# Layer 0 of a four-layer graph network: the set-up and the block chains of the scatter places in small steps, matmuls and adds one turn behind their inputs

## The chip, the cores and the metric

The kernel runs on one core of a Trainium2 chip. The metric is the device time in microseconds of one execution; three runs of the kernel before give 11480.86 us as the median (11465.4 to 11503.06).

## The reference

Four graph layers over 6250 nodes with 128 features and 200000 edges. Each layer normalizes the nodes, gathers rows by one end of an edge, and sums what it made of them at the other end. Layer 0, which the change touches:

```python
h = jnp.maximum(_layernorm(x, axis=-1), 0.0)
agg = jax.ops.segment_sum(h[src], dst, num_segments=6250)     # edge_index = stack([src, dst])
x = x + jax.nn.relu((h + agg) @ W1 + b1) @ W2 + b2
```

Edges come sorted by `dst`. Layer 1 sums by `src` instead, so its messages must be put in the order of `src`.

## The kernel before

**The windows of layer 0** (`windows0`, L795 to L832). The edges are cut into NG = 391 groups of FT = 4 tiles of 128. As `dst` is sorted, a group touches a window of at most FW = 64 nodes. For each group g, POOL gathers four tiles of rows of `h_tab` by `src` with indirect DMAs (`gather`, L298) into one of the buffers of `m` (pool `eg`, 6); DVE makes the one-hot rows of the edges' places in the window (`hot`, L822); PE adds up the group with four f32 matmuls, eight passes in the profile (`ps`, L825, 3 PSUM buffers); and DVE adds `ps` into `acc` at the window's start (L827), which it has in a register that is loaded for eight groups at a time (`starts`, L608).

**The places for layer 1** (`ranks`, L613 to L793) are computed in the same stretch. It is a Python generator: after each group, `windows0` calls it for a number of turns (L828): one for g below 20, then two and three by turns. It finds for each edge its place in a stable order by `src // 32` (NB = 196 bins), as follows. (1) Constants and shifted ids. (2) Fourteen turns that count all bins: each makes two wide one-hot tiles `hot_h` (L663, 128 x 1792) and has 14 matmuls on them (L666). (3) Steps on small tiles: the counts are folded, go through memory (`c_tab`, L690 and L691), are scanned (L694), and give each group's first bin (L707 to L728), with matmuls between. (4) 820 turns over the 782 pairs of tiles. `sums(q)` makes the pair's one-hot rows `hot_b` (L744, two DVE instructions) and adds them into the block's `sizes` with a matmul (L746). A block is RB = 32 pairs. After its last pair, `before_tiles` (L749 to L772) runs the block's chain in one turn: DVE copies the sizes (L752, L753), PE makes the counts before each tile and the running total (L755 to L762), DVE splits them into three bf16 pieces (L764 to L771). `places(q)` comes 38 turns after `sums(q)`: PE makes the pair's places in PSUM (`pq`, L778 and L779, 2 buffers), and DVE picks and sums each row's own with `hot_b` (L782, two instructions with a read of the sum after each).

**What sets the order.** Each engine works through its own queue in order. The framework orders instructions when the program is built, near the order of the source, and inserts the waits. In the built program DVE has L827 of a group behind the L782 of the group's first turn and ahead of the L744 of its second; PE has a pair's L746 two turns behind its L744, just ahead of a later pair's L778.

Of the kernel before, what the change touches and what calls it, by code (L numbers as in the profile page):

```python
# [9 lines left out]
F32 = mybir.dt.float32  # L10
I32 = mybir.dt.int32
BF16 = mybir.dt.bfloat16
# [8 lines left out]
D = 128  # L21
# [34 lines left out]
def bcast(col, n):  # L56

    p, g = col.shape
    return col.unsqueeze(2).to_broadcast([p, g, n])
# [9 lines left out]
def gnn_kernel(ctx: ExitStack, tc: tile.TileContext, t, out):  # L69
# [543 lines left out]
    def ranks(st, src):  # L613
# [6 lines left out]
        bp = st.enter_context(tc.tile_pool(name="rb", bufs=RB + RLAG + 2))  # L620
        wp = st.enter_context(tc.tile_pool(name="rw", bufs=3))
        qp = st.enter_context(tc.tile_pool(name="rq", bufs=1, space=PSUM))
        rp = st.enter_context(tc.tile_pool(name="rr", bufs=2, space=PSUM))
# [3 lines left out]
        sh = kp.tile([P, n], I32, name="sh")  # L627
# [30 lines left out]
        yield  # L658
        count = qp.tile([P, HK, 16], F32, name="count")
        for b in range(0, n8, HN):  # L660
            hot = hp.tile([P, 2, HN, 16], BF16, name="hot_h")
            for k in range(2):
                nc.vector.tensor_tensor(hot[:, k], lanes[:, :16].unsqueeze(1).to_broadcast([P, HN, 16]),  # L663
                                        bcast(parts[:, k, b:b + HN], 16), op=ALU.is_equal)
            for i in range(0, HN, HK):
                nc.tensor.matmul(count, hot[:, 0, i:i + HK, :].rearrange("p k l -> p (k l)"),  # L666
                                 hot[:, 1, i:i + HK, :].rearrange("p k l -> p (k l)"),
                                 start=(b + i == 0), stop=(b + i == n8 - HK))
            yield
# [8 lines left out]
        nc.vector.tensor_scalar(mask, lanes[:, :HK], own_f[:, 0:1], None, op0=ALU.is_equal)  # L678
        diag = kp.tile([P, HK, 16], F32, name="diag")
# [3 lines left out]
        fold = kp.tile([P, 16], F32, name="fold")  # L683
        nc.vector.tensor_scalar(fold, lanes[:, :16], own_f[:, 1:2], None, op0=ALU.is_equal)
        pr = qp.tile([16, 16], F32, name="count")
        nc.tensor.matmul(pr, fold, by_hi, start=True, stop=True)
        sizes = kp.tile([16, 16], F32, name="sizes")
        nc.vector.tensor_copy(sizes, pr)
        cr = kp.tile([1, 3, NB], F32, name="cr")
        nc.sync.dma_start(c_tab[0].rearrange("(h l) -> h l", l=16), sizes)  # L690
        nc.sync.dma_start(cr[:, 0, :], c_tab[0:1, 0:NB])  # L691
        yield
        nc.vector.memset(cr[:, 2, :], 0.0)
# [4 lines left out]
        nc.tensor.matmul(pr, ones[0:1, :], cr[:, 1, :], start=True, stop=True)  # L698
        ends = kp.tile([P, NB], F32, name="ends")
        nc.vector.tensor_copy(ends, pr)  # L700
        bin_ = kp.tile([P, 2, 4], F32, name="bin_")
        for k in range(2):
            for c in range(4):
                le = wp.tile([P, NB], F32, name="junk")
                at = wp.tile([P, 1], F32, name="at")
                nc.vector.tensor_scalar(at, pid, float(FE), float(c * P * FE + k * (FE - 1)), op0=ALU.mult,
                                        op1=ALU.add)  # L707
                nc.vector.tensor_scalar(le, ends, at, None, op0=ALU.is_le)
                nc.vector.tensor_reduce(bin_[:, k, c:c + 1], le, axis=AX.X, op=ALU.add)
        yield  # L710
        by_group = kp.tile([1, 2, 4 * P], F32, name="by_group")
        for k in range(2):
            pr = qp.tile([1, 4 * P], F32, name="count")
            for c in range(4):
                nc.tensor.matmul(pr[:, c * P:(c + 1) * P], bin_[:, k, c:c + 1], ident, start=True, stop=True)
            nc.vector.tensor_copy(by_group[:, k, :], pr)
# [9 lines left out]
        nc.tensor.matmul(pr, ones[0:1, :], by_group[:, 0, :NG], start=True, stop=True)  # L726
        nc.vector.tensor_copy(base_b, pr)
        yield  # L728
        pos_f = kp.tile([P, n], F32, name="pos_f")
        sofar = cr[:, 2, :]  # L730
        hots, pieces = {}, {}
# [4 lines left out]

        def sums(q):

            b, i = divmod(q, RB)
            if i == 0:  # L740
                hots["ps"] = qp.tile([RB, 2, NB], F32, name="sizes")
            hot = hots[q] = bp.tile([P, 2, NB], BF16, name="hot_b")
            for k in range(2):
                nc.vector.tensor_scalar(hot[:, k, :], lanes_b, bins[:, 2 * q + k:2 * q + k + 1], None,  # L744
                                        op0=ALU.is_equal)
            nc.tensor.matmul(hots["ps"], at_pair[:, RB - i:2 * RB - i], hot, start=(i == 0),  # L746
                             stop=(i == RB - 1 or q == n // 2 - 1))

        def before_tiles(b, sofar):  # L749

            c = hp.tile([RB, 2, NB], F32, name="c")
            nc.vector.tensor_copy(c[:, 0, :], hots["ps"][:, 0, :])  # L752
            nc.vector.tensor_tensor(c[:, 1, :], c[:, 0, :], hots["ps"][:, 1, :], op=ALU.add)  # L753
            pb = qp.tile([3 * RB, 2, NB], F32, name="before")
            nc.tensor.matmul(pb, earlier[:, 0].rearrange("p k q -> p (k q)"), twice(c[:, 1, :]), start=True,  # L755
                             stop=False)
            nc.tensor.matmul(pb, ones[0:1, :3 * RB], twice(sofar), start=False, stop=False)
            nc.tensor.matmul(pb[:, 1, :], earlier[:, 1].rearrange("p k q -> p (k q)"), c[:, 0, :],
                             start=False, stop=True)
            pt = qp.tile([1, NB], F32, name="count")  # L760
            nc.tensor.matmul(pt, ones[:RB, 0:1], c[:, 1, :], start=True, stop=False)
            nc.tensor.matmul(pt, ones[0:1, 0:1], sofar, start=False, stop=True)  # L762
            sofar = hp.tile([1, NB], F32, name="sofar")
            nc.vector.tensor_copy(sofar, pt)  # L764
            r = hp.tile([3 * RB, 2, NB], F32, name="r")
            v = pieces[b] = hp.tile([3 * RB, 2, NB], BF16, name="pieces")
            nc.vector.tensor_copy(v, pb)
            nc.vector.scalar_tensor_tensor(r, v, part[:, 0:1], pb, op0=ALU.mult, op1=ALU.add)
            nc.vector.tensor_copy(v, r)
            nc.vector.scalar_tensor_tensor(r, v, part[:, 1:2], r, op0=ALU.mult, op1=ALU.add)  # L770
            nc.vector.tensor_copy(v, r)  # L771
            return sofar  # L772

        def places(q):
            b, i = divmod(q, RB)
            hot = hots.pop(q)
            pq = rp.tile([P, 2, NB], F32, name="pq")
            nc.tensor.matmul(pq, pick[:, i:i + 1].to_broadcast([3 * RB, P]), pieces[b], start=True, stop=False)  # L778
            nc.tensor.matmul(pq, below, hot, start=False, stop=True)  # L779
            for k in range(2):  # L780
                junk = wp.tile([P, NB], F32, name="junk")
                nc.vector.tensor_tensor_reduce(junk, pq[:, k, :], hot[:, k, :], 1.0, 0.0, ALU.mult, ALU.add,  # L782
                                               pos_f[:, 2 * q + k:2 * q + k + 1])

        for q in range(n // 2 + RB + RLAG):
            if q < n // 2:
                sums(q)
            if q % RB == RB - 1 and q < n // 2 or q == n // 2 - 1:
                sofar = before_tiles(q // RB, sofar)
            if 0 <= q - RB - RLAG:  # L790
                places(q - RB - RLAG)
            yield
        nc.vector.tensor_copy(pos, pos_f)  # L793

    def windows0():  # L795

        with ExitStack() as st:
# [3 lines left out]
            with ExitStack() as st:  # L801
                lp = st.enter_context(tc.tile_pool(name="ld", bufs=1))
                gp = st.enter_context(tc.tile_pool(name="eg", bufs=6))
                wp = st.enter_context(tc.tile_pool(name="ew", bufs=4))
                pp = st.enter_context(tc.tile_pool(name="ep", bufs=3, space=PSUM))
# [3 lines left out]
                di = lp.tile([P, NG * FT], I32, name="di")  # L809
                nc.sync.dma_start(di, t["dst_f"])  # L810
                loc = lp.tile([P, NG, FT], F32, name="loc")
                nc.vector.tensor_copy(loc, di.rearrange("p (g j) -> p g j", j=FT))
                nc.vector.tensor_tensor(loc, loc, bcast(base, FT), op=ALU.subtract)
# [3 lines left out]
                for g in range(NG):  # L817
                    m = gp.tile([P, FT, D], F32, name="m")
                    for j in range(FT):
                        gather(m[:, j, :], h_tab, src[:, g * FT + j:g * FT + j + 1])  # L820
                    hot = wp.tile([P, FT, FW], F32, name="hot")
                    nc.vector.tensor_tensor(hot, lane, bcast(loc[:, g, :], FW), op=ALU.is_equal)  # L822
                    ps = pp.tile([P, FW], F32, name="ps")
                    for j in range(FT):
                        nc.tensor.matmul(ps, m[:, j, :], hot[:, j, :], start=(j == 0), stop=(j == FT - 1))  # L825
                    a = acc[:, bass.ds(starts(g, DVE), FW)]
                    nc.vector.tensor_tensor(a, a, ps, op=ALU.add)  # L827
                    for _ in range(1 if g < 20 else 3 if g % 2 else 2):  # L828
                        next(rank, None)
                for _ in rank:  # L830
                    pass
# [745 lines left out]
```

## Time and profile before

| | us |
|---|---|
| runs: median (lowest to highest) | 11480.9 (11465.4 to 11503.1) |
| the profiled execution | 11639.2, span 11637.5 |
| layer 0's windows: first gather to last add L827 | 78.1 to 2457.5 |
| last L782 of the places | 2235.3 |
| TensorE clock granted over the span | 0.54 |

Busy time, engine by engine (share of the span, instructions), and the span in 40 slices of 291 us, each digit a busy share in tenths:

```profile
PE 8422.1 (72%) x32097; PEld 6515.2 (56%) x32097; DVE 5839.1 (50%) x23079; ACT 1506.2 (13%) x3279; POOL 6132.0 (53%) x6269
...
PE   3788888659998889989983666666663466566666
...
DVE  4455555323343434344434666666665355555555
...
PEclk9555555555555555555555555555555555655555
```

Layer 0's windows are the first eight slices or so: PE is at seven to eight tenths, no engine at nine, and after the first slice the granted clock is half. A row of the profile has the line, the engine, what it writes and reads, the count, and then the busy time, the mean in ns, the idle time just ahead of it on its engine, and what ended most of that. "Issue" is idle time with no wait that the profile shows; "remote" is a wait whose end the profile can't put down to an instruction of this core. Queue entries (POOLq, SPq) are not counted as busy.

### The profile page before, as it was taken

Reading aid. Unit: us, or ns where it says so; the run is one execution under the profiler, and the core shown is the slowest. Engines: PE = TensorE matmul, PEld = TensorE weight load, DVE = VectorE, ACT = ScalarE, POOL = GpSimd, SP = SyncE. Lnnn points to the kernel's source line nnn. Section 1 sums busy time; section 2 is a strip of 40 time slices with the busy share of each in tenths; the row PEclk is TensorE's granted clock in tenths of the full one; section 3 lists DMA queues with packets and bytes.
Section 4 is the critical chain, followed back from the end, with each engine's and each line's share of the span. In section 5 each row is a group of like instructions: output and inputs, shape, how many; then the busy total and the mean of one; then the engine's idle time right before and its main releaser. Section 6 shows DMA issues by size and latency. Waiting matters only on the chain.

```text
span 11637.5 us, 118951 instructions
## 1 busy us (share of the span) xinstructions
PE 8422.1 (72%) x32097; PEld 6515.2 (56%) x32097; DVE 5839.1 (50%) x23079; ACT 1506.2 (13%) x3279; POOL 6132.0 (53%) x6269
## 2 busy tenths in 40 slices
PE   3788888659998889989983666666663466566666
PEld 2444444446666556669953666666663465555555
DVE  4455555323343434344434666666665355555555
ACT  0000000014343334331110000000001010011101
POOL 5666666625665666640006555555551556555662
PEclk9555555555555555555555555555555555655555
DMA  2111111113333333335512222222221233333332
GB/s 65 44 44 44 44 43 44 44 55 93 93 93 92 95 92 95 93 104 158 158 64 60 65 66 64 65 66 63 66 63 62 80 88 88 86 86 88 88 87 81
DMA packets 457356, 893.32 MB, mean 77 GB/s; under 512 B 149642, under 2 KB 231743, under 8 KB 455763
## 3 DMA queue, kind: packets, MB, share of 16 engines
q1 hardware_dynamic: 245552, 456.89, 14.0%
q0 software_dynamic: 200192, 412.80, 12.6%
q10 hardware_dynamic: 10918, 15.65, 0.4%
q8 instruction: 281, 4.60, 0.2%
q14 instruction: 413, 3.38, 0.1%
HBM read 753.95 MB, written 130.80 MB: 76 GB/s over the span
## 4 chain that ended last, share of the span: by engine, by line
PE 30%; issue 8%; DVE 8%; another core or an unknown queue 8%; POOL 4%; ACT 1%; DMA 1%; DVEq 0%; ACTq 0%; POOLq 0%; SPq 0%
PE ps L959 6%; PE pz L1354 4%; PE pz L1073 4%; POOL m L298 4%; PE ps L1401 4%; PE ps L1153 3%; PE pw L905 1%; PE pf L896 1%; PE py L899 1%; DVE z L1358 1%; DVE z L1078 1%; PE ps L1154 1%; PE ps L1402 1%; DVE hot L1396 1%
## 5 line engine op out<-in xcount | busy, mean ns | idle before, releaser
L298 POOL DMA_INDIRECT m<-l_tab,src x1564 | 1522.2, 973 | 1242.7 <-issue 563.1
L302 POOL DMA_INDIRECT m_tab<-m,pos x1564 | 1569.4, 1003 | 1152.5 <-issue 576.2
L298 POOL DMA_INDIRECT m<-g_tab,dst x1564 | 1499.6, 959 | 1068.0 <-PE ps L1401 426.4
L298 POOL DMA_INDIRECT m<-h_tab,src x1564 | 1538.5, 984 | 849.5 <-issue 412.2
L1401 PE MATMUL ps<-hot,m 128*128 128x64 f32 x3128 | 736.7, 399 | 676.5 <-DVE hot L1396 351.8
L1153 PE MATMUL ps<-hot,m 128*128 128x64 f32 x3128 | 787.9, 420 | 486.6 <-issue 265.6
L1401 PEld LDWEIGHTS ps<-hot,m 128*128 128x128 f32 x3128 | 685.8, 310 | 720.3 <-DVE hot L1396 368.6
L1153 PEld LDWEIGHTS ps<-hot,m 128*128 128x128 f32 x3128 | 724.2, 327 | 550.0 <-issue 295.3
L1073 PE MATMUL pz<-win,hotT 65*128 65x128 f32 x3128 | 825.2, 441 | 277.9 <-DVE hotT L1070 136.8
L1354 PE MATMUL pz<-win,hotT 128*128 128x128 f32 x3128 | 786.7, 415 | 275.1 <-issue 183.9
L825 PEld LDWEIGHTS ps<-hot,m 128*128 128x128 f32 x3128 | 736.1, 326 | 391.9 <-issue 177.6
L899 PEld LDWEIGHTS py<-win,hotT 64*128 64x128 f32 x3128 | 676.2, 316 | 478.6 <-issue 426.3
L825 PE MATMUL ps<-hot,m 128*128 128x64 f32 x3128 | 732.5, 410 | 264.9 <-DVE hot L822 116.5
L909 DVE TENSOR_TENSOR m<-pw,L_gnn_b_f_b 128x512 f32<-128x512 f32 x391 | 269.7, 690 | 1259.6 <-PE pw L905 382.7
L905 PEld LDWEIGHTS pw<-L_gnn_W_f,sp_r 128*128 128x128 f32 x3128 | 683.9, 321 | 380.7 <-issue 334.3
L905 PE MATMUL pw<-L_gnn_W_f,sp_r 128*128 128x128 f32 x3128 | 800.6, 435 | 121.7 <-DVE sp_r L931 86.1
L1073 PEld LDWEIGHTS pz<-win,hotT 65*128 65x128 f32 x3128 | 713.4, 330 | 308.2 <-issue 153.9
L899 PE MATMUL py<-win,hotT 64*128 64x128 f32 x3128 | 785.4, 428 | 118.8 <-issue 106.3
L1354 PEld LDWEIGHTS pz<-win,hotT 128*128 128x128 f32 x3128 | 673.8, 308 | 298.4 <-issue 276.2
L896 PE MATMUL pf<-row_a,L_gnn_W_f 20*128 20x512 f32 x782 | 770.3, 1090 | 37.2 <-ACT sp_r L918 15.0
L959 PE MATMUL ps<-hot,m 128*128 128x64 f32 x3128 | 671.0, 420 | 18.7 <-DMA m<-m_tab 18.4
L959 PEld LDWEIGHTS ps<-hot,m 128*128 128x128 f32 x3128 | 671.4, 333 | 21.0 <-ACT ids L962 18.7
(315 smaller groups left out, 11881.8 us busy)
## 6 DMA issues: line engine op xcount, KB each, us to landing
m<-m_tab SPq DMA_DIRECT2D x391, 262.0 KB
row<-in_dst_row SPq DMA_DIRECT2D x390, 256.0 KB
row<-e_tab SPq DMA_DIRECT2D x390, 256.0 KB
row_w<-in_w_row SPq DMA_DIRECT2D x195, 256.0 KB
m<-h_tab,src POOLq DMA_INDIRECT x1564
m_tab<-m,pos POOLq DMA_INDIRECT x1564
m<-l_tab,src POOLq DMA_INDIRECT x1564
m<-g_tab,dst POOLq DMA_INDIRECT x1564
```

What stands on the lines that cost most here:

```text
L298: nc.gpsimd.indirect_dma_start(out=dst, out_offset=None, in_=table[:], in_offset=bass.IndirectOffsetOnAxis(ap=idx, axis=0))
L302: nc.gpsimd.indirect_dma_start(out=table[:], out_offset=bass.IndirectOffsetOnAxis(ap=idx, axis=0), in_=src, in_offset=None, **kw)
L825: nc.tensor.matmul(ps, m[:, j, :], hot[:, j, :], start=(j == 0), stop=(j == FT - 1))
L896: nc.tensor.matmul(pf, w_f1, row["a"][:, es], start=True, stop=True)
L899: nc.tensor.matmul(py[:, j, :], hot[:, j * P:(j + 1) * P], w, start=True, stop=True)
L905: nc.tensor.matmul(pw[:, j, :], sp[:, j * P:(j + 1) * P], w_f2, start=True, stop=True)
L909: nc.vector.tensor_tensor(v, pw, b_f2b.unsqueeze(1).to_broadcast([P, FT, D]), op=ALU.add)
L959: nc.tensor.matmul(ps, m[:, j, :D], hot[:, j, :], start=(j == 0), stop=(j == FT - 1))
L1073: nc.tensor.matmul(pz[:, j, :], hot[:, j * P:(j + 1) * P], w, start=True, stop=True)
L1153: nc.tensor.matmul(ps[:, 0, :], m[:, j, :], hot[:, j, :], start=(j == 0), stop=(j == FT - 1))
L1354: nc.tensor.matmul(pz[:, j, :], hot[:, j * P:(j + 1) * P], w, start=True, stop=True)
L1401: nc.tensor.matmul(ps[:, 0, :], m[:, j, :], hot[:, j, :], start=(j == 0), stop=(j == FT - 1))
```

## The change

Nothing is computed in another way; steps move between turns, and buffers change.

- `windows0`: in iteration g, POOL's gathers and `hot` of group g, then the turns, then the matmuls of group g - 1, then the add of group g - 2; two iterations more. `eg` 7 buffers instead of 6, `ps` 2 instead of 3. One turn up to g = 35 instead of 19. The `dst` ids land in `loc` itself, and the cast ahead of the subtraction (L812) is gone.
- Set-up: constants (`fold`, the eight `at` columns, the zeroed row of `cr`) move ahead of the counting; the counting's matmuls are a turn behind their `hot_h`; the small steps stand in 12 turns instead of 3, with three turns between the two table DMAs and the scan.
- Pairs: DVE makes `hot_b` of pair q, PE adds the sizes of pair q - 1, the block's chain goes on by one step a turn (four steps), PE makes `pq` of pair q - 38, and DVE picks the places from the `pq` of the turn before. `pq` has 3 buffers instead of 2, `hot_b` one more.

Turns in all: 838 before (the last ones after group 347), 849 after (group 361). The core of the diff:

```diff
-        bp = st.enter_context(tc.tile_pool(name="rb", bufs=RB + RLAG + 2))
+        bp = st.enter_context(tc.tile_pool(name="rb", bufs=RB + RLAG + 3))
...
-        rp = st.enter_context(tc.tile_pool(name="rr", bufs=2, space=PSUM))
+        rp = st.enter_context(tc.tile_pool(name="rr", bufs=3, space=PSUM))
...
+        hot = None
+        for b in range(0, n8 + HN, HN):
+            if hot is not None:
+                for i in range(0, HN, HK):
+                    nc.tensor.matmul(count, hot[:, 0, i:i + HK, :].rearrange("p k l -> p (k l)"),
+                                     hot[:, 1, i:i + HK, :].rearrange("p k l -> p (k l)"),
+                                     start=(b + i == HN), stop=(b + i == n8 + HN - HK))
+            if b < n8:
+                hot = hp.tile([P, 2, HN, 16], BF16, name="hot_h")
...
         nc.sync.dma_start(cr[:, 0, :], c_tab[0:1, 0:NB])
-        yield
-        nc.vector.memset(cr[:, 2, :], 0.0)
+        for _ in range(3):
+            yield
         nc.vector.tensor_tensor_scan(cr[:, 1, :], cr[:, 0, :], cr[:, 2, :], 0.0, ALU.add, ALU.add)
...
             nc.tensor.matmul(pt, ones[0:1, 0:1], sofar, start=False, stop=True)
+            yield
             sofar = hp.tile([1, NB], F32, name="sofar")
             nc.vector.tensor_copy(sofar, pt)
...
             nc.vector.scalar_tensor_tensor(r, v, part[:, 0:1], pb, op0=ALU.mult, op1=ALU.add)
+            yield
             nc.vector.tensor_copy(v, r)
             nc.vector.scalar_tensor_tensor(r, v, part[:, 1:2], r, op0=ALU.mult, op1=ALU.add)
+            yield
             nc.vector.tensor_copy(v, r)
...
-        for q in range(n // 2 + RB + RLAG):
-            if q < n // 2:
-                sums(q)
-            if q % RB == RB - 1 and q < n // 2 or q == n // 2 - 1:
-                sofar = before_tiles(q // RB, sofar)
-            if 0 <= q - RB - RLAG:
-                places(q - RB - RLAG)
+        for q in range(pairs + RB + RLAG + 1):
+            new = found
+            if q < pairs:
+                hots[q] = rows_of(q)
+            if 0 < q <= pairs:
+                sums(q - 1)
+            if q % RB == 0 and 0 < q < pairs or q == pairs:
+                chain = before_tiles((q - 1) // RB)
+            if chain is not None:
+                chain = chain if next(chain, 0) is None else None
+            if 0 <= q - RB - RLAG < pairs:
+                found = q - RB - RLAG, before_pair(q - RB - RLAG)
+            else:
+                found = None
+            if new is not None:
+                places(*new)
             yield
...
-                gp = st.enter_context(tc.tile_pool(name="eg", bufs=6))
+                gp = st.enter_context(tc.tile_pool(name="eg", bufs=7))
...
-                pp = st.enter_context(tc.tile_pool(name="ep", bufs=3, space=PSUM))
+                pp = st.enter_context(tc.tile_pool(name="ep", bufs=2, space=PSUM))
...
+                one_, two_ = None, None
+                for g in range(NG + 2):
+                    new = None
+                    if g < NG:
...
+                        nc.vector.tensor_tensor(hot, lane, bcast(loc[:, g, :], FW), op=ALU.is_equal)
+                        new = m, hot
+                    for _ in range(1 if g < 36 else 3 if g % 2 else 2):
                         next(rank, None)
+                    last_ = two_
+                    if one_ is not None:
+                        m, hot = one_
+                        ps = pp.tile([P, FW], F32, name="ps")
+                        for j in range(FT):
+                            nc.tensor.matmul(ps, m[:, j, :], hot[:, j, :], start=(j == 0), stop=(j == FT - 1))
+                        two_ = ps
+                    if g > 1:
+                        a = acc[:, bass.ds(starts(g - 2, DVE), FW)]
+                        nc.vector.tensor_tensor(a, a, last_, op=ALU.add)
+                    one_ = new
```

## The prediction

> **What bounds the kernel now.** I read the page first (which part of the span is layer 0), then the busy table by stretches, then the waits of the layer's main stretch engine by engine, and last a short piece of the timeline. The change touches layer 0's windows only, and these run from the first gather at 78.1 us to the last add at 2457.5 us. The table by stretches (us, PE, PEld, DVE, ACT, POOL busy, granted clock, DMA):
>
> ```profile
> 78.00:200.00 122.00, 56.06 (x322) 50.01 (x322) 76.20 (x81) 0.00 (x0) 102.35 (x65) 1.00 0.12 36
> 200.00:400.00 200.00, 116.34 (x386) 68.65 (x386) 69.23 (x344) 0.00 (x0) 131.51 (x137) 0.68 0.16 45
> 400.00:2200.00 1800.00, 1481.63 (x4815) 777.90 (x4816) 927.28 (x5186) 0.00 (x0) 1133.34 (x1184) 0.51 0.15 44
> 2200.00:2460.00 260.00, 114.33 (x424) 93.24 (x422) 36.74 (x158) 0.00 (x0) 171.26 (x179) 0.50 0.17 48
> ```
>
> No engine is full in the main stretch: PE is idle for 318 of 1800 us, DVE for half. 296 groups pass there (1184 gathers by 4), 6.08 us each. The page's row of the gathers gives the floor of the layer:
>
> ```profile
> L298 POOL DMA_INDIRECT m<-h_tab,src x1564 | 1538.5, 984 | 849.5 <-issue 412.2
> ```
>
> An undisturbed gather is 0.944 us (the line's median) and 0.305 us of issue, 1.249 in all, so a group needs 4 x 1.249 = 5.0 us, and 1564 gathers need 1953 of the 2376 us that they take. What is over, 423 us, is 62 in gathers longer than 0.944 and some 360 in POOL waiting, nearly all for a buffer of `m`, that is for PE. So PE's idle time is the question. The groups of the main stretch (busy, mean ns | idle before, and what ended it):
>
> ```profile
> L825 PE MATMUL ps<-hot,m 128*128 128x64 f32 x2376 | 533.9, 404 | 25.2 <-DVE hot L822 22.7 <-DVE c L752 2.5
> ...
> L778 PE MATMUL pq<-pieces,pick 96*128 96x392 bf16 x741 | 373.9, 505 | 60.7 <-DVE pos_f L782 42.3 <-PE pq L779 3.0 <-PE sizes L746 1.8
> L746 PE MATMUL sizes<-hot_b,at_pair 128*32 128x392 bf16 x718 | 358.0, 501 | 232.4 <-DVE hot_b L744 213.6 <-issue 16.2 <-DVE acc L827 2.2
> ...
> L827 DVE TENSOR_TENSOR acc<-acc,ps 128x64 f32 x296 | 65.4, 221 | 654.6 <-PE ps L825 303.7 <-remote 228.4 <-PE pq L779 116.6
> ...
> L767 DVE CAST pieces<-before 96x392 bf16<-96x392 f32 x24 | 13.5, 562 | 56.8 <-PE before L758 55.2 <-issue 1.7
> ```
>
> PE's 318 us stand before L746, L778 and L825, and 213.6 of them wait for L744's rows. But L744 waits for nothing itself: it is queued on DVE behind the add L827, and there DVE stands 654.6 us for PE. How that goes round, in the timeline:
>
> ```profile
> 999.20 0.22 DVE L827 TENSOR_TENSOR acc<-acc,ps 128x64 f32 x1 [4.49 <-remote]
> 999.34 0.45 DVE L744 TENSOR_SCALAR hot_b<-lanes_b,bins 128x196 bf16<-128x196 bf16 x2
> 999.44 0.98 POOL L298 DMA_INDIRECT m<-h_tab,src  x1 [2.61 <-remote]
> ...
> 999.84 0.49 PE L746 MATMUL sizes<-hot_b,at_pair 128*32 128x392 bf16 x1 [3.56 <-DVE hot_b L744]
> ...
> 1000.41 0.51 PE L778 MATMUL pq<-pieces,pick 96*128 96x392 bf16 x1
> ...
> 1000.71 0.53 PE L779 MATMUL pq<-hot_b,below 128*128 128x392 bf16 x1
> ...
> 1001.17 0.51 PE L746 MATMUL sizes<-hot_b,at_pair 128*32 128x392 bf16 x1
> ```
>
> DVE waits 4.49 us at the add; only then come L744, then PE's L746 (3.56 us idle) and POOL's next gather (2.61). "Remote" is a wait of which the profile names no cause: PE had issued all of it, and its count reached DVE late. 50 adds of the stretch wait so, 228.4 / 50 = 4.6 us each.
>
> **PE's own floor.** Starts in a row without a wait: L746 to L778 0.44, L778 to L779 0.30, L779 to L746 0.46, so 1.20 us a turn; the eight L825 of a group take 1.74 from the first to the next L746 (1007.17 to 1008.91). With 2.5 turns a group, and 0.14 less where L825 follows L779: 3.00 + 1.74 - 0.14 = 4.60. A block's chain holds PE 4.9 us (1021.69 to 1026.58) once in 32 turns, 12.8 groups: 0.38. Together 4.98 us, as much as the gathers' 5.0. The excess of 6.08 over 5.0, 1.08 x 296 = 320, is both PE's 318 and the gathers' (1800 - 1184 x 1.249 = 321): one loss, seen twice.
>
> **The change part by part.**
> The adds of the windows, L827. The add now takes the sums of the group before last, whose matmuls were issued an iteration earlier, some 5 us. In the built order at least three turns of PE's work lie between the two. The waits for L825 (303.7) and L779 (116.6) end, and L744 behind them is early. The late counts remain as a fact, but at the add they are covered (4.6 against 5).
>
> The places, L778 to L782. DVE takes at turn q the pair that PE made at q - 1, and three `pq` buffers let PE go on two turns, 2.4 us, when DVE stands still. A late count of 4.6 us now stops DVE at L782, and PE after 2.4 us, or after 2.4 + 1.74 if a window is among the two turns. So 50 x 0.5 to 50 x 2.2 us of PE's idle time stay; I take the middle, 1.3, so 65.
>
> The block's chain in four steps: DVE no longer waits 55.2 at L767 (and 18.0 at the `sofar` copy) with L744 queued behind; the work itself is the same. I keep 30 us for what is late next, the double load of PE in a chain's turn (4.9 + 3 us against six groups of gathers in stock, so mostly hidden). PE's idle time in the stretch goes from 318 to 95, and a group from 6.08 to 5.0 + 95 / 296 = 5.32 us: 296 x 0.76 = 225 us.
>
> Stretch 78 to 200: the 28 L663 stay, and gathers over them take 1.575 us on the mean (102.35 / 65). POOL sets the pace there: gain nothing. 200 to 400: 137 gathers need 171 of 200 us; the set-up's steps (two long waits of the add, 10.96 and 22.88 us, one for the table's round through memory) get turns of their own, and groups 20 to 36 get one turn instead of 2.5. I take 20 of the 29. After 2200: 179 gathers need 224 of 260; the adds wait there 11 to 21 us for late counts, and POOL with seven buffers is stopped less: 10 of the 36, less 4 since the turns now last to group 361 instead of 347. The cast L812 (0.91 us) goes: 1. Moved constants (`fold`, `at`, the memset) are the same instructions at 0.1 to 0.2 us beside gathers: nothing, and if uncovered 3 us. The two table DMAs keep their queue with nothing behind them; their landing has three turns, which are three groups and 15 us, instead of one. The dst load goes to another tile on the same queue: nothing.
>
> Sum: 225 + 20 + 10 - 4 + 1 = 252. On the profiled execution 11639.2 (span 11637.5) becomes 11387. It stands 1.4% over the median of the runs shown, 11480.9; in that proportion 252 is 249, so 11232.
>
> **Two rules against rows.** The row first: in the main stretch 1184 gathers are busy 1134 us, 958 ns each against 944, 17 us over in all, beside 1436 L744 of 272 ns. The Trainium skill, "SBUF — State Buffer", section "Who interferes with whom", says that a tensor_scalar in a two-port mode holds the port pair which GpSimd needs, and blocks it fully. By the rule a denser DVE costs up to all of L744, 327.5 us, and the change would lose; by the row 17 us stay 17, at most 20 when packed into 5.32 / 6.08 of the time. I take the row. Second, the clock: 0.51 in the main stretch with PE 82% busy, and 0.50 to 0.53 from 2800 to 4600 us with PE 90% busy (1619.6 of 1800). "TensorE: Matmul & The Clock Gate", section on the HAM clock gate, says that sustained activity releases the full clock. By the rule a PE with fewer gaps would be twice as fast and the gathers alone would bind, a gain of about 365; the denser stage denies it here, so I take 0.51.
>
> **The rivals.** (a) Forecast, 11232, chance 0.62. (b) The gathers alone bind: late counts hide wholly or the clock rises. Gain 318 + 29 + 20 = 367, scaled 362: 11119; 0.10. For it: both floors are 5.0. Against: two engines at one floor, with turns of 2 and 3, never pack fully. (c) The late counts keep their full price: the 228 us of remote waits reach PE through L782 instead of L827. Gain 318 - 228 = 90, with 20 in the other stretches 110: 11372; 0.14. For it: in the timeline above one late count stops three engines. (d) The built order was already overlapped (L746 stood two turns behind L744 before), so nothing moves: 11480; 0.06. Against: L827's 654.6. (e) Slower. PE's L825 now needs the add of two groups back (two `ps` buffers, was three), and that add sits at the end of an iteration behind two L782. A count late by more than one group, like the 11.2 and 21.1 us after 2200, stops PE 5 us sooner and the add, L782 and L744 behind it. It decides from 50 such stops of 5 us, which eat the 250; with one in every third of the 325 groups under turns, 108 x 5 = 540 less 250: 290 slower, with half of them 11500; 0.08.
>
> **How the numbers follow.** A measurement tells 0.3%, 34 us. Faster: (a), (b) and (c), 0.86; same: (d), 0.06; slower: (e), 0.08. The range takes in (b) mostly and (c): 11125 to 11405. Its ends are PE's idle time fully gone and a gain of 75.
>
> **What would show it.** After: the add without waits over 1 us in the main stretch; PE's idle before the sizes matmul under 60 us per 1800; gathers' start to start nearer 1.33 than 1.52; last gather near 2205 us; granted clock still 0.5; gathers still 958 ns. I am wrong if DVE's waits turn up in full at the places' sums, if the gathers lengthen, or if PE waits for the window's add.

## The result, and the profile after

After takes 11433.8 us (median of 8 runs, 11426.0 to 11453.5), before 11485.2 beside it (8 runs): a ratio of 0.9951, with a 95% interval of 0.994 to 0.9961. That is 51 us faster, where 249 were forecast, and above the range. The profiled execution is an ordinary one this time (11446.6, span 11444.9). That of before, 11639, was 1.3% over its own runs, in stages that the change doesn't touch as well, so of the 193 us between the two spans only the 83 us of layer 0's gathers bear on the change: first to last gather 2375.1 us before (78.1 to 2453.2), 2291.6 after (78.2 to 2369.9). Part of these is the slower execution as well: its later stages with indirect transfers, where both kernels have the same code, are 1.2 to 2.6% longer than those of after.

The table by stretches, to be laid beside that of before (PE, PEld, DVE, ACT, POOL busy, clock):

```profile
78.00:200.00 122.00, 63.51 (x333) 52.78 (x334) 78.60 (x97) 0.00 (x0) 100.75 (x70) 0.64 0.15 39
200.00:400.00 200.00, 95.67 (x332) 65.44 (x333) 47.91 (x206) 0.00 (x0) 134.38 (x140) 0.50 0.18 46
400.00:2200.00 1800.00, 1481.12 (x4970) 795.35 (x4969) 955.28 (x5342) 0.00 (x0) 1179.74 (x1232) 0.53 0.17 46
2200.00:2460.00 260.00, 148.71 (x591) 118.47 (x590) 45.52 (x147) 7.37 (x12) 119.62 (x125) 0.56 0.16 44
```

PE's idle time in the main stretch, the whole subject of the forecast, is 1800 - 1481.1 = 318.9 us. Before it was 318.4. 308 groups pass instead of 296 (5.84 us each, from 6.08), but PE stands as long as it did; the twelve groups more show in its busy time, 1481.1 / 308 = 4.81 us a group instead of 1481.6 / 296 = 5.01, of which the forecast had said nothing. The groups of that stretch, with the answers to the rows shown of before (busy, mean ns | idle before, and what ended it):

```profile
L298 POOL DMA_INDIRECT m<-h_tab,src x1232 | 1180.3, 958 | 620.6 <-issue 316.7 <-remote 139.9 <-PE ps L863 100.9
L863 PE MATMUL ps<-hot,m 128*128 128x64 f32 x2461 | 538.4, 396 | 5.9 <-DVE acc L867 5.9
L802 DVE CUSTOM_DVE_ANT_0 junk<-pq,hot_b 128x196 f32<-128x196 f32 x1531 | 488.4, 353 | 615.4 <-remote 366.3 <-PE ps L863 116.9 <-PE pq L795 106.4
L794 PE MATMUL pq<-pieces,pick 96*128 96x392 bf16 x765 | 382.1, 499 | 244.8 <-remote 132.1 <-DVE pos_f L802 102.7 <-issue 3.8
L760 PE MATMUL sizes<-hot_b,at_pair 128*32 128x392 bf16 x739 | 363.2, 496 | 25.6 <-DVE hot_b L751 21.7 <-DVE r L784 2.1 <-remote 1.6
L867 DVE TENSOR_TENSOR acc<-acc,ps 128x64 f32 x307 | 65.4, 213 | 16.1 <-remote 11.6 <-issue 2.8 <-PE pq L795 1.6
```

(L802, L794, L760, L867 and L863 are L782, L778, L746, L827 and L825 of before.) Two rows of before are not shown yet:

```profile
L298 POOL DMA_INDIRECT m<-h_tab,src x1184 | 1134.0, 958 | 667.0 <-issue 317.6 <-PE ps L825 148.6 <-remote 130.9
L782 DVE CUSTOM_DVE_ANT_0 junk<-pq,hot_b 128x196 f32<-128x196 f32 x1483 | 470.7, 353 | 112.1 <-PE ps L825 75.7 <-PE pq L779 24.0 <-PE sizes L746 4.5
```

DVE's 655 us of waits have left the add, where 16 remain, and most of them stand at the places' sums, 615 us from 112, 366 of them remote. PE's idle time has left the sizes matmul (232 to 26) and stands at the first places matmul (61 to 245). In all, DVE is idle for 845 us of the stretch instead of 873, and PE as long as before. The waits moved, and hardly any went away. The question is what they are.

### The profile page after: what moved, and what is told of

Same layout as the page of the kernel before. It is cut to its first block, busy times and chain, and to the rows that moved or that the text cites. A ratio compares the mean times of both kernels' runs of the same rounds, so it can differ in the third digit from the quotient of the medians.

```text
span 11444.9 us, 118934 instructions
## 1 busy us (share of the span) xinstructions
PE 8383.8 (73%) x32097; PEld 6516.8 (57%) x32097; DVE 5834.5 (51%) x23078; ACT 1503.3 (13%) x3279; POOL 6129.3 (54%) x6269
## 4 chain that ended last, share of the span: by engine, by line
PE 44%; DVE 8%; another core or an unknown queue 8%; issue 8%; POOL 2%; ACT 1%; DMA 1%; DVEq 0%; ACTq 0%; SPq 0%; POOLq 0%
PE ps L998 6%; PE pz L1112 6%; PE ps L1192 5%; PE pz L1393 5%; PE pw L944 5%; PE pf L935 4%; PE py L938 4%; PE ps L1440 4%; POOL m L298 2%; PE ps L1193 2%; DVE z L1117 1%; PE ps L1441 1%; DVE z L1397 1%; DVE z L1114 1%
## 5 line engine op out<-in xcount | busy, mean ns | idle before, releaser
L1440 PEld LDWEIGHTS ps<-hot,m 128*128 128x128 f32 x3128 | 692.9, 313 | 614.4 <-issue 289.8
L1192 PEld LDWEIGHTS ps<-hot,m 128*128 128x128 f32 x3128 | 724.0, 327 | 520.9 <-issue 303.3
L863 PEld LDWEIGHTS ps<-hot,m 128*128 128x128 f32 x3128 | 730.2, 322 | 419.2 <-issue 237.1
L863 PE MATMUL ps<-hot,m 128*128 128x64 f32 x3128 | 717.7, 403 | 282.1 <-DVE acc L867 99.1
L802 DVE CUSTOM_DVE_ANT_0 junk<-pq,hot_b 128x196 f32<-128x196 f32 x1564 | 498.7, 353 | 630.9 <-remote 379.6
```

Source lines behind the costliest of these rows:

```text
L1192: nc.tensor.matmul(ps[:, 0, :], m[:, j, :], hot[:, j, :], start=(j == 0), stop=(j == FT - 1))
L1440: nc.tensor.matmul(ps[:, 0, :], m[:, j, :], hot[:, j, :], start=(j == 0), stop=(j == FT - 1))
```

## The experiments

**Each half alone, a second turn of cover, and no turns between the groups.** Four kernels on one chip.

windows_only keeps the places of before and takes the new order of the windows. Against the kernel after, its windows differ in one line:

```diff
-                    for _ in range(1 if g < 36 else 3 if g % 2 else 2):
+                    for _ in range(1 if g < 20 else 3 if g % 2 else 2):
```

> Only the group's half of the change: one-hots and matmuls one turn behind their inputs, the add two groups back, seven gather buffers, two PSUM tiles for the windows; the places keep the order of before (one turn per group up to group 20). If late counts of PE set the pace (first theory), the add's 655 us of waits fall under 50, but the same counts are now awaited at the places' sums (L782's successor), which follow their matmuls in the same turn: its waits grow to 500 us or more, cadence 5.8 to 6.1 us a group, 11,420 to 11,490 us. If the order at the add was what cost (rival), a third or more of the forecast 225 us comes: under 11,400 us.

places_only is the other half:

> Only the places' half: set-up and chain in small steps, matmuls of the places one turn ahead of their sums, one turn per group up to group 36; the windows keep the order of before, add directly behind its matmuls. First theory (late counts): hot_b's wait on PE (232 us) goes, the add still waits for each late count, 11,440 to 11,490 us. Rival (PE's wait for hot_b was the real loss): most of the 51 us of the whole change or more is here, 11,380 to 11,440 us.

deep, on top of the kernel after:

```diff
-        rp = st.enter_context(tc.tile_pool(name="rr", bufs=3, space=PSUM))
+        rp = st.enter_context(tc.tile_pool(name="rr", bufs=5, space=PSUM))
-            new = found
+            new, found = found, later
-                found = q - RB - RLAG, before_pair(q - RB - RLAG)
+                later = q - RB - RLAG, before_pair(q - RB - RLAG)
```

> The kernel after with the places' sums two turns behind their matmuls instead of one: five pq tiles in PSUM (the set-up's and the chain's tiles take turns in the same five), one more hot_b tile. First theory (the counts come late, PE's work itself is on time): two turns are about 5 us of cover against delays of 4.6 to 6.1 us, so most of the 348 us of remote waits at the sums go, and PE's 226 us in front of the first places matmul with them; cadence from 5.84 to 5.4 us or less, 11,230 to 11,330 us. Rival (PE's array itself is late, so that the recorded ends are too early and the counts are right): the same waits stand somewhere else, cadence 5.75 to 5.9, 11,410 to 11,450 us.

serial:

```diff
-                    for _ in range(1 if g < 36 else 3 if g % 2 else 2):
-                        next(rank, None)
+                    if g < 1:
+                        next(rank, None)
```

> The kernel after with no turn of the ranks beside the groups: all of them after the last window, so the overlap is gone. The windows alone: gathers' floor of 5.0 us a group, 391 groups 1,955 us; the turns alone at 1.9 to 2.2 us (three DVE passes and two sums against 1.2 us of PE), 822 of them 1,560 to 1,800 us; about 1,200 to 1,500 us slower than after. If late counts belong to PE's semaphores whatever the load (first theory), the adds in the windows alone (one group, 5 us, of cover) still show remote waits of 5 us or more, some 10 in each 200 us or fewer, and the cadence is 5.1 to 5.5 us. If they come of PE's load or of an array that is late (rival), at PE's 35 per cent there are none: 5.0 us a group.

Measured, with before at 10085.7 us beside them: windows_only 10082.7, ratio 0.9999 (0.9991 to 1.0008); places_only 10081.4, 0.9997 (0.9988 to 1.0005); deep 10093.1, 1.0009 (1.0001 to 1.0018); serial 10524.5. No expectation holds, because before itself is 12% faster here, and the four traces have not a single remote wait. (serial, one run, did not put all turns behind the windows either: the framework moved them forward, so that the first places matmul stands at 802 us.)

**Before and after on another chip.**

> The kernel before, unchanged, for a second profile. If late counts (waits that the profile puts down to remote) belong to the kernel, as the forecast took for granted, some 50 adds of the main stretch wait 4.6 us each again, the cadence is 6.1 us a group and the time 11,480 us. If they belong to the chip or the moment of the first comparison, as the 10,086 us of before beside the last four kernels suggest, there are next to none, the cadence is 5.1 us, set by the gathers, and the time is 10,090 us.

> The kernel after, unchanged. Without late counts the gathers bind in both kernels and the change is worth nothing: 0.998 to 1.002 of before, windows' waits at the sums under 100 us in 1300, cadence 5.1 us. With late counts on this chip it is 0.994 to 0.996 as in the first comparison. Rival (order of the queues): 0.975 to 0.99 wherever it runs.

> The places' sums two turns behind their matmuls, once more. On a chip with late counts: the second turn covers most of the 4.6 to 6.1 us, 0.978 to 0.988 of before; if the array itself is late instead, 0.994 to 0.997, as the kernel after. Without late counts: 1.000 to 1.002 of before, as the first time.

Before 10090.1 us, after 10095.9, ratio 1.0006 (0.9997 to 1.0014), deep_again 1.0009 (1.0001 to 1.0017). So there are two kinds of chips; all runs on one chip were of one kind. (No chip was met at two times, so "kind of chip" may as well be the state that a chip was in.) On the first kind (the first comparison and four later chips) before takes 11475 to 11693 us; on the second (three chips) 10086 to 10090. The time from the first to the last gather or scatter of each stage (the plain loads: from the last scatter to the next gather), from the four profiles, in us:

| stage | before, first kind | after, first kind | before, second kind | after, second kind |
|---|---|---|---|---|
| layer 0, gathers | 2375 | 2292 | 2010 | 2024 |
| layer 1, scatters | 2545 | 2514 | 2325 | 2309 |
| layer 1, plain loads | 922 | 927 | 928 | 928 |
| gathers of `l_tab` | 2614 | 2584 | 2233 | 2233 |
| gathers of `g_tab` | 2506 | 2443 | 1981 | 1981 |

Every stage with indirect transfers is 9 to 27% longer on the first kind; the one without is the same. Before on the second kind, 400 to 1700 us:

```profile
L298 POOL DMA_INDIRECT m<-h_tab,src x1033 | 985.8, 954 | 314.8 <-issue 251.4 <-PE ps L825 22.9 <-DMA m<-h_tab,src 19.2
L825 PE MATMUL ps<-hot,m 128*128 128x64 f32 x2063 | 451.1, 392 | 14.5 <-DMA m<-h_tab,src 13.9
L778 PE MATMUL pq<-pieces,pick 96*128 96x392 bf16 x645 | 315.9, 490 | 14.7 <-DVE pos_f L782 10.8
L746 PE MATMUL sizes<-hot_b,at_pair 128*32 128x392 bf16 x645 | 313.0, 488 | 27.8 <-DVE hot_b L744 27.7
L827 DVE TENSOR_TENSOR acc<-acc,ps 128x64 f32 x258 | 57.2, 222 | 424.8 <-PE ps L825 424.8
```

This is the old order, undisturbed. The add waits 425 us in 1300 (588 in 1800, against 655), and it costs nothing: PE is 96% busy, the gathers run at 1300 / 1033 = 1.26 us, and a group takes 5.03 us. DVE waits for PE because PE has the more work; that is DVE's spare time, not a loss. Both floors of the forecast (5.0 us for the gathers, 4.98 for PE) agree with this, and on these chips before stands on them already.

**Late counts made on purpose.** In before, and in the same way on a pair's `pq` in after and in deep:

```diff
+                    if g % 6 == 0 and 40 < g < 356:
+                        nc.scalar.copy(slow[:, :FW], ps)
+                        for _ in range(9):
+                            nc.scalar.copy(slow, slow)
+                        nc.vector.tensor_copy(seen, slow[:, :1])
```

> Late counts made on purpose, in the kernel before: in every sixth group from 42 to 354 (53 of them) ScalarE, idle here, reads the window's sums and then copies a 128x512 tile onto itself nine times, some 6.3 us, and VectorE reads the last of it just ahead of the add, so PE's result counts as late for the add and all behind it (the dst ids also land without the cast, for room; the output is unchanged). First theory (DVE standing at the add stops PE and then the gathers, one loss): with late counts before lost 366 us over 71 of them, 5.2 us each, so 53 cost 180 to 280 us where there are none otherwise, 10,270 to 10,370 us. Rival (the loss comes by POOL, which waits for PE's counts itself, and DVE's wait is only beside it): here POOL's counts are on time, so under 50 us.

> The same delay in the kernel after, put on the pq of every 15th pair (52 of them), ahead of the places' sums. First theory: one turn of cover, so 3 to 5 us each are left, 150 to 250 us over the same kernel without them, less than before_late by 30 to 100. By the forecast's own step (1.3 us each) 70 us. Rival (POOL): under 50 us.

> The same delay in the kernel with the places' sums two turns behind their matmuls. First theory: about 5 us of cover against 6.3, so 1 to 2 us each at the sums and less at PE, 0 to 80 us over the same kernel without them. If the cover of a second turn does nothing, as much as after_late.

This chip was of the first kind: before 11636.8; before_late 11644.7, 1.001 (0.9999 to 1.002); after_late 11575.3, 0.9943 (0.9925 to 0.996); deep_late 11584.0, 0.9949 (0.9928 to 0.9969). The waits for ScalarE in before_late's and deep_late's traces (us in all, times, longest):

```profile
DVE acc L834 <- ACT slow L829: 105.1, 30, 9.9
```

```profile
DVE seen L808 <- ACT slow L802: 121.1, 38, 8.6
```

before_late takes 8 us more (-1 to 23), where 180 to 280 were expected. But its waits for ScalarE are no addition: between 400 and 2100 us the add waits 620 us in all, in before 618. The framework put `seen` up to two turns later, and DVE often came late anyway. So the run doesn't tell what a late count at the add costs, and the theory that it was made for, that a DVE that stands stops PE and then the gathers, is not tested by it. A second turn of cover brings nothing that can be seen: deep_late is no better than after_late.

**More of PE's work in stock, less work for PE, both.** wide adds to deep:

```diff
+            p = q - 2
-            if 0 < q <= pairs:
-                sums(q - 1)
+            if 0 < p <= pairs:
+                sums(p - 1)
...
-                        ps = pp.tile([P, FW], F32, name="ps")
+                        ps = pools[0].tile([P, FW], F32, name="pq")
```

> More of PE's own work in stock: the kernel with the sums two turns behind, and besides hot_b three turns ahead of its first matmul (was one) and the windows' sums in one ring of seven PSUM tiles with pq, where they had two of their own. On a chip with remote waits (the chip of the first comparison, 11,485 us, and of the delays made on purpose, 11,637): if the loss of 366 us is PE running dry while DVE waits for a count (first theory), PE now has some 5 us of work without DVE and most of it comes back, 0.972 to 0.985 of before; if no order of the queues covers it (rival), 0.993 to 0.997, as the kernel after. On a chip without them (10,090 us): 0.999 to 1.002.

quarter changes the kernel after:

```diff
-                        for j in range(FT):
-                            nc.tensor.matmul(ps, m[:, j, :], hot[:, j, :], start=(j == 0), stop=(j == FT - 1))
+                        nc.tensor.matmul(ps, m[:, FT - 1, :], hot[:, FT - 1, :], start=True, stop=True)
```

> The kernel after with one of each group's four tile matmuls (the other three tiles are left out of the sums), so PE has 1.3 us less to do in a group, 3.7 instead of 5. Without remote waits the gathers bind alone: the stage stays at 2,010 to 2,025 us. With them: if a full PE that can't catch up is what makes them cost (first theory), the stage falls from 2,290 to some 2,050 to 2,100 us; if they stop the gathers or the whole core (rival), it stays at 2,250 or more.

wide_quarter is wide with the same edit:

> The kernel wide (sums two turns behind, hot_b three ahead, one ring of seven PSUM tiles) with one of each group's four tile matmuls (three tiles are left out of the sums). On a chip with remote waits: quarter alone left the stage at 2,265 us and wide alone at 2,284. If the loop between PE and DVE paces the stage (first reading), a light PE with deep rings takes the stage to 2,020 to 2,120 us; if the gathers are struck themselves (rival), 2,240 or more. Without remote waits: 2,010 to 2,025.

> The kernel after with no turn called between the groups. On a chip with remote waits: the first 600 us then hold almost only gathers, four matmuls, one one-hot and one add a group. If gathers are struck on their own (rival), these groups take 5.5 us or more as well; if the loop between PE and DVE over the places is what is struck (first reading), 5.0 to 5.2 us until the places begin. Without remote waits: last gather at 2,087 us as the first time.

All on chips of the first kind; quarter, wide_quarter and serial_again ran once each, and the first two leave three of each group's four tiles out of the sums. wide: 11406.3 against 11474.6, 0.9942 (0.993 to 0.9955), gathers' stage 2284 us (after: 2292). quarter: 2265 us, though PE is busy only 61% of the time (1034.9 of 1700). wide_quarter: 2294 us. serial_again: 2259, and its early part, 200 to 800 us, almost without places, has 412 gathers in 600 us, 5.83 us a group; serial on the second kind had 445, 5.39. So neither cover, nor a light PE, nor the absence of the places brings the 2010 us back.

**What POOL waits for.** The traces of the first kind agree on one thing. POOL is idle for over 0.5 us ahead of a gather 120 times in before (321 us between 400 and 2100), 104 times in after (263), 94 in wide (240), 81 in quarter (234); on the second kind never, in either kernel. A group's first gather waits until PE has read the buffer for the last time, in the matmuls of the group six back (seven in after). So the trace tells whether PE was behind with these matmuls, or done with them and only its count (the semaphore's, by which it tells POOL so) not yet there. All stops over 0.5 us of layer 0, without those of the first groups, in us (times):

| | matmul ended within the last 1 us | matmul ended over 1 us earlier |
|---|---|---|
| before | 145 (42) | 257 (106) |
| after | 41 (10) | 278 (112) |
| before_late | 170 (43) | 238 (99) |
| after_late | 57 (15) | 302 (111) |
| quarter | 74 (21) | 201 (72) |
| serial_again | 0 | 268 (82) |

At the stops of the second column the matmul had ended 3.0 us before the gather began in before, 7.9 in after (medians). So most of POOL's stops are no waits for PE's work, nor for DVE behind it: PE's count itself comes late to POOL. The forecast's own timeline holds such a stop. The gather at 999.44 us had waited 2.61 us, and the last matmuls on its buffer are these:

```profile
993.27 1.81 PE L825 MATMUL ps<-hot,m 128*128 128x64 f32 x8
```

They ended at 995.07 us, before POOL stopped (996.83). DVE's add, which went on at 999.20, had waited for the same matmuls.

**The gathers cut off from PE.**

```diff
+                m0 = lp.tile([P, FT, D], F32, name="m0")
+                for j in range(FT):
+                    gather(m0[:, j, :], h_tab, src[:, j:j + 1])
-                        new = m, hot
+                        new = m0, hot
```

> The kernel after, with every window's matmuls reading the tile of group 0 (all other sums are left out of the output), so the gathers of the other groups are read by nobody and wait only for their own buffers' transfers; PE's and DVE's work and their waits for each other stay. On a chip without remote waits: last gather at 2,030 to 2,100 us, as before. On a chip with them: if POOL stops only because PE and DVE are behind (first reading: the loop between PE and DVE), the gathers run through and the last one stands at 2,030 to 2,110 us; if POOL is stopped on its own account, by its transfers' counts (rival), it stays at 2,250 or more.

free also has six buffers of `m` again. First kind, one run: 12782.5 us against 11663.8. The gathers ran through, but at 1.40 us (1600 / 1143), so the last stands at 2295 us; that is in the rival's range, but not for its reason, as POOL is not stopped and each gather is longer (1067 ns). PE and DVE all but stopped. Between 400 and 2000 us:

```profile
L298 POOL DMA_INDIRECT m<-h_tab,src x1143 | 1219.2, 1067 | 381.2 <-issue 381.2
L866 PE MATMUL ps<-hot,m 128*128 128x64 f32 x344 | 81.1, 417 | 391.0 <-issue 391.0
L802 DVE CUSTOM_DVE_ANT_0 junk<-pq,hot_b 128x196 f32<-128x196 f32 x114 | 36.8, 359 | 886.3 <-remote 857.7 <-issue 28.6
L794 PE MATMUL pq<-pieces,pick 96*128 96x392 bf16 x60 | 30.5, 509 | 871.2 <-remote 768.5 <-DVE pos_f L802 69.6 <-DVE r L784 26.4
```

POOL waits for no count, and 53 sums wait 16.2 us each for a `pq` that is ready. 60 turns pass in 1600 us. The first three pairs, in the timeline:

```profile
943.06 0.53 PE L795 MATMUL pq<-hot_b,below 128*128 128x392 bf16 x1
...
944.27 0.53 PE L795 MATMUL pq<-hot_b,below 128*128 128x392 bf16 x1
...
945.47 0.53 PE L795 MATMUL pq<-hot_b,below 128*128 128x392 bf16 x1
...
1006.65 0.36 DVE L802 CUSTOM_DVE_ANT_0 junk<-pq,hot_b 128x196 f32<-128x196 f32 x1 [63.71 <-remote]
...
1015.75 0.36 DVE L802 CUSTOM_DVE_ANT_0 junk<-pq,hot_b 128x196 f32<-128x196 f32 x1 [7.62 <-remote]
...
1023.73 1.09 POOL L298 DMA_INDIRECT m<-h_tab,src  x1 [0.30 <-issue]
1024.15 0.36 DVE L802 CUSTOM_DVE_ANT_0 junk<-pq,hot_b 128x196 f32<-128x196 f32 x1 [7.38 <-remote]
...
1024.86 0.51 PE L794 MATMUL pq<-pieces,pick 96*128 96x392 bf16 x1 [7.13 <-DVE pos_f L802]
```

PE ended the three pairs at 943.6, 944.8 and 946.0 us; DVE could sum them from 1006.65, 1015.75 and 1024.15 on. The counts come in order, one at a time, 63 to 78 us late. For the 54 waits at the sums over 2 us the lateness is 22 to 78 us, 50 on the mean, and 51 of them end 0.4 to 0.6 us after the start of a gather. The other direction is prompt: PE's 75 waits over 2 us end 0.06 us (median) after the end of a DVE instruction. What is late is PE's count on its way to DVE, while gathers are issued without a break.

> The same kernel as free, for a control (the windows' matmuls all read group 0's tile, the sums of the others are left out; gathers are read by nobody). Where it ran first, with remote waits, gathers ran through at 1.40 us and PE and DVE all but stood: places' sums 16 us late each, done 1,480 us after the last gather's stage instead of 190. On a chip without remote waits, if it is that chip's trouble (first theory): no such starving, last gather at 2,030 to 2,100 us and the turns done within 100 us of it, 10,000 to 10,250 us in all. If it is the kernel's own order (rival): starved here too, over 11,000 us. On a chip with remote waits: as the first time, 12,700 to 12,900 us.

The same kernel on the second kind, one run: 10154.9 us against 10087.0, last gather 2138 us. The same stretch:

```profile
L298 POOL DMA_INDIRECT m<-h_tab,src x1259 | 1218.3, 968 | 383.7 <-issue 383.7
L866 PE MATMUL ps<-hot,m 128*128 128x64 f32 x2456 | 518.2, 389 | 0.0
L802 DVE CUSTOM_DVE_ANT_0 junk<-pq,hot_b 128x196 f32<-128x196 f32 x1382 | 443.1, 354 | 290.4 <-PE pq L795 288.8
L794 PE MATMUL pq<-pieces,pick 96*128 96x392 bf16 x690 | 335.6, 486 | 0.0
```

**A pause of POOL in each group**, in the kernel free:

```diff
+                        nc.gpsimd.iota(idle, pattern=[[1, 1024]], base=0, channel_multiplier=0,
+                                       allow_small_or_imprecise_dtypes=True)
```

> The kernel free with a pause of POOL in each group: one iota over a 128x1024 tile that nobody reads, some 1.2 us by the 0.35 us of the 128x256 one. On a chip with remote waits: if counts between PE and DVE get through when POOL stops issuing gathers (first theory), PE and DVE keep up with the groups: gathers 391 x (5.6 + 1.3) = 2,700 us, the next stage begins at 2,800 to 3,000 us instead of 3,775. If a pause of POOL doesn't help (rival): later than 3,700 us. Without remote waits: 391 x 6.3, some 2,450 to 2,550 us for the gathers, with the turns done beside them.

> The kernel paced once more, in the hope of a chip with remote waits. There, if a pause of POOL lets PE's and DVE's counts through (first theory): PE and DVE keep up with the groups, and the next stage begins at 2,700 to 3,000 us, against 3,775 in free; if it doesn't (rival): later than 3,700 us. On a chip without remote waits: 10,450 to 10,490 us, as the first time.

One run each. paced, second kind: 10470.6 us, gathers' stage 2386 us. paced_again, first kind: 11658.6 against 11692.9 of before (which has all its sums), gathers' stage 2386 us, to the microsecond the same, and the next stage begins at 2654 us, where it began at 3776 in free. On the first kind:

```profile
L298 POOL DMA_INDIRECT m<-h_tab,src x1076 | 1039.3, 966 | 289.4 <-issue 289.4
L869 PE MATMUL ps<-hot,m 128*128 128x64 f32 x2560 | 529.5, 383 | 0.2 <-DVE acc L873 0.2
L802 DVE CUSTOM_DVE_ANT_0 junk<-pq,hot_b 128x196 f32<-128x196 f32 x1450 | 466.8, 360 | 216.9 <-PE pq L795 134.6 <-issue 63.3 <-remote 14.8
L794 PE MATMUL pq<-pieces,pick 96*128 96x392 bf16 x723 | 347.2, 480 | 25.9 <-DVE pos_f L802 11.2 <-remote 6.2 <-issue 4.5
```

1.0 us of POOL (the iota's mean is 1004 ns) in each group takes the remote waits at the sums from 858 to 15 us and PE's idle time at L794 from 871 to 26. So on the first kind PE's counts get through once the gathers leave breaks. Whether it is the issue or the transfers in flight that hold them back is not told apart: a pause stops one and thins the other. Nor was a shorter pause tried in the kernel after, which waits for its gathers; 1.0 us in each of 391 groups costs as much as the loss.

## Why the prediction was wrong

**The floors** (5.0 us of gathers, 4.98 of PE) hold: 5.03 and 5.10 us a group on the second kind, before and after.

**The step that failed** is where PE's idle time was made the whole question: POOL waits "nearly all for a buffer of `m`, that is for PE. So PE's idle time is the question", and "one loss, seen twice". The two sums agreed (318 and 321 us), but POOL's wait is mostly not for PE's work. Of the 402 us of POOL's stops in the table above, PE was behind in 145; in 257 it had been done with the buffer for over 1 us, and POOL itself waited for the late count. The new order of PE's and DVE's work did reach the first kind of stop, 145 to 41 us, but the stops for late counts went from 257 to 278. Together that is the 83 us between the two traced stages, and after_late against before_late, on one chip, shows the same pattern (170 to 57, 238 to 302). Nor did the seventh buffer help: it lets POOL ask a group later, and the counts were later by as much, 7.9 us instead of 3.0. Rival (c) had seen that "one late count stops three engines", but priced it only by way of L782.

**The price of the late counts** was wrong with it: "So 50 x 0.5 to 50 x 2.2 us of PE's idle time stay; I take the middle, 1.3, so 65", and "PE's idle time in the stretch goes from 318 to 95". I took the number and the length of the late counts as fixed and asked what a turn of cover hides. Measured: 60 remote waits at the sums, 6.1 us each, in place of 50 of 4.6, and 318.9 us of PE's idle time. Two turns (deep_late, with its added delays) or three of `hot_b` with seven PSUM tiles (wide) do no better: 0.9949 and 0.9942. free shows how far a count can slip when POOL waits for none, 50 us on the mean. In the kernels themselves 49 of the 50 remote waits at the add of before end while POOL stops, though POOL stops for 19% of the stretch, and 45 of the 60 at the sums of after (15%), in both 2.4 us after the stop began (median). That fits with counts that come through when the gathers pause, but doesn't prove it there, as POOL often waits for that same count; what is shown by a change is free against paced_again.

**L744 behind the add** was not the cause either. On the second kind the same order has 28 us before L746 in 1300, and a group at 5.03.

**The add** was right: 655 us of waits fell to 16, and before the sizes matmul 232 to 26. But a wait of DVE was taken for a cost, and 425 of 1300 us cost nothing where no count is late.

**The other stretches.** 78 to 200: 70 gathers instead of 65, nothing was forecast. 200 to 400: 140 instead of 137, where 20 us, some 16 gathers, were forecast. The last gather is at 2370 instead of 2205, and start to start in 400 to 2100 it is 1.46 us (1700 / 1164), nearer the old 1.52 than 1.33.

**The two rules** came out as the rows said: gathers 958 ns as before, clock 0.53. (Whether L744 runs in a two-port mode at all, no run here shows.)

**The rivals.** (c), the late counts keep their price, is nearest, with 110 against 51 us (here; 62 in after_late with its delays, 68 in wide). (b), the gathers alone bind, is true on the second kind, but for before as well, so its gain is nil. (e) does not happen: L863 waits 5.9 us for the add. (d), nothing moves, is the result on the second kind, though not for its reason. What the 51 us of the first kind are is told by POOL's stops, as above; why a PE that is less behind leaves more late counts is open. Each half alone ran on the second kind only.

## What to carry to other kernels

An engine that waits long for another one is no loss while the other is full; ask first whether the busiest engine stands, and what for. Where an engine waits for a buffer, look up when the last reader ended: if it was long done, a new order of the reader's work had little to gain here. A wait whose end no record of the core explains must not be carried into the new order as a fixed number of fixed length: find out what holds it (here a stretch with the gathers cut loose, and one with a pause) before counting on a cover for it. And take the profile on a second chip before a queue's order is blamed.

## What the runs showed of the hardware

- Chips of two kinds: 11475 to 11693 and 10086 to 10090 us for the same program, and 1491 of the 1543 us between the two spans of before lie in the stages with indirect transfers. What sets the kinds apart is open. The traces of the first kind also lack records of semaphore events where gathers run, and none in the plain loads: layer 0 of before has 10356 of them against 30819 on the second kind, the plain loads of layer 1 10176 on both. paced_again has 16459 of paced's 29722 and hardly a remote wait, so missing records alone are not the stop; whether the recording of the events has a part in the late counts, no run here tells.
- On the first kind PE's counts reach DVE 50 us late on the mean under unbroken gathers (the 54 waits over 2 us), one at a time, and DVE's reach PE in 0.06 us. PE's counts to POOL are late as well: 7.9 us at the median of after's 112 stops.
- A gather under unbroken issue takes 1.067 us on the first kind and 0.968 on the second.
- In serial the granted clock is 1.00 from 400 to 1700 us with PE 77% busy (1002.7 of 1300), and the window's matmuls take 444 ns each, against 392 in before on the second kind at a clock of 0.55 with PE 96% busy.
